# One group of expert tiles, a vector add in the recurrence, and routing one pair later in a two-layer hybrid model

## The chip, the cores and the metric

The kernel runs on one core of a Trainium2 chip. The metric is device time in microseconds (us) of one execution. Three executions took 5005.71, 4992.72 and 5005.48 us, so the median is 5005.48 us. One further execution was profiled; it took 4976.55 us, and its span from the first to the last instruction is 4974.8 us. A profile tells of five engines: PE (TensorE, matrix products), DVE (VectorE), ACT (ScalarE), POOL (GpSimd) and SP (SyncE, which here only issues transfers). PEld is the loading of weights for PE.

## The reference

Sixteen samples go through a tokenizer and two layers; all data are float32, and a row has 256 values. After the tokenizer each sample has 569 tokens (441 from its image, 128 of text).

- Tokenizer: a 2x2 convolution with stride 2, then one attention over 441 image tokens.
- Layer 0: attention in windows of 64 tokens with 8 heads, then a mixture of 8 experts. Each token goes to its two best experts (256 to 512 to 256, with gelu), weighted by the softmax of the router.
- Layer 1: a phasor attention (phases of keys and queries, a running sum over the tokens, a layer norm), then an LSTM of 256 units over the 569 tokens, one after the other, with a gated prefix and suffix sum of its output.

The LSTM is the part that can't be done in parallel over tokens:

```
gates = xp + h @ W_hh.T            # xp = x @ W_ih.T + biases, known for all tokens ahead
i, f, g, o = split(gates, 4)
c = sigmoid(f) * c + sigmoid(i) * tanh(g)
h = sigmoid(o) * tanh(c)
```

## The kernel before, in words

Samples are handled in 8 pairs, `p` = 0 to 7. The 2x569 tokens of a pair fill 9 chunks of 128 rows; chunk `c` and `4 + c` hold the same 128 token times of the two samples, and chunk 8 holds the first 32 and the last 25 tokens of both.

**Tokenizer** (lines 169 to 319), then **windows** (lines 452 to 544). For each pair, rows are normalized and transposed into a tile `xT` (`normed_columns`, line 146), then come Q, K and V (L462 to L488), the attention of each chunk (L495 to L534), and the output row block (L537 to L542). After each pair `send_rows(p)` (line 358) routes its rows: it normalizes again (L141, into `XN` and into `xT`, of which the pool holds one buffer for both uses), forms router scores (L365), ranks them on DVE (L370 to L421), and scatters every row to the two expert regions in HBM by 18 indirect transfers from POOL (L424).

**Experts** (`experts(g)`, line 617). The chunks are dealt into groups: `GROUPS = [[8], [0, 4], [1, 5], [2, 6, 3, 7]]`. In each group every expert's rows are cut into tiles of 256 rows, the number of tiles being a bound that holds for any routing: 15, 23, 23 and 39, so 100 in all. A tile loads its rows and 1154 KB of one expert's weights, transposes (L696, L700), and does two products with gelu between (L707, L713, L717, L722). Its result goes to HBM tensor `YS[g]`.

**Phasors** (`phasors(i)`, line 928) are a generator per pair of chunks: `front` (line 768) gathers the two expert rows of each token (L777, POOL, from `YS` of the group), adds them, normalizes, and forms phases and values; after four pairs a sine on ACT; then `back` (line 839) does the phasor attention, a layer norm, and the LSTM's input part (L916, L920), which goes to the HBM tensor `XPD` of a block. `phasors(8)` does the first 32 tokens and keeps the last 25 for `last_tokens`; `phasors(i)` does the 128 tokens of LSTM block `i + 1`. A `front` or `back` of `phasors(0)` to `phasors(3)` handles two chunks, one of `phasors(8)` and `last_tokens` handles one.

**LSTM** (`lstm(j)`, line 1069). Blocks have 32, 128, 128, 128, 128 and 25 tokens. Eight tokens are a unit: `steps` (line 966) loads `xp` for the unit and runs its 8 steps, and `sums_of` (line 1022) afterwards does the prefix sums and the output of the unit. The four quarters of the units lie in four strips of 32 partitions, so gates are a 128x256 tile. In one step:

1. `begin(t)` (L977): PE multiplies `xp` by the identity into the PSUM tile `g`. It is issued for step `t + 1` right after the recurrent product of step `t`.
2. L989: eight matrix products of `h` with `W_hh` add to it.
3. L996 and L998: ACT reads `g` and makes tanh of the gates.
4. L1000, L1005, L1010, L1012: DVE forms the cell and transposes it and the output gate.
5. L1014: ACT, tanh of the cell. L1015: DVE makes the new `h` (tile `X`). Then step 2 of the next token.

**Order.** A scheduler in the language's library places all instructions ahead of time; each engine then runs its list in order and waits at an instruction until what it needs is there. Steps have high priority, and other work is placed between them. The code says what may lie beside what: `run_all` takes turns between the generators given to it, and what one `run_all` emits may be placed beside the `lstm` emitted next to it.

```
run_all(tiles(0))
run_all((phasors(8), 2 * NP), tiles(1))
lstm(0)
run_all((phasors(0), 2 * NP), tiles(2))
lstm(1)
run_all((phasors(1), 2 * NP), tiles(3))
lstm(2)
```

## Time and profile before

| what | value |
|---|---|
| median of 3 executions | 5005.48 us |
| profiled execution: time, span | 4976.55 us, 4974.8 us |
| PE busy | 3956.3 us, 80% of the span |
| DVE busy | 2287.5 us, 46% |
| ACT, POOL busy | 1173.8 us, 1193.8 us |
| mean granted clock of PE | 0.915 |
| first expert tile done (start of its last add, L722) | 1577.1 us |
| last scatter of rows (L424) begins | 1545.3 us |
| first and last new `h` (L1015) | 2006.0 us, 4876.2 us |

In the page, times are counted from the first instruction. A busy time is the sum over an engine's instructions, and a group's line gives tile names as output, then inputs. The chain of waits is a list of what released what, from the last instruction backwards. PEclk is the share of the full clock that PE was granted. In the list of instructions in order of time, the columns are start, duration, engine, line, operation, output and inputs, and in brackets the idle time before it and what ended it.

### The profile page before, as it was taken

To read this page: it belongs to the slowest core of one execution; us is meant where nothing else is said; L and a number is where in the kernel's file an instruction comes from. 1 tells how busy PE (TensorE), PEld (TensorE's weight loads), DVE (VectorE), ACT (ScalarE), POOL (GpSimd) and SP (SyncE) were. 2 spreads that over 40 slices of the span, in tenths; PEclk is the share of its full clock that TensorE was granted. 3 is DMA by queue.
4 is the path that set the end of the run, shared out by engine and by line. 5 is a ranking of instruction groups with operands and counts; after the bars stand their busy time and mean duration, and the time that the engine had idled before them with its cause. 6 is when DMAs were issued, how large, how long until landed. Compare 5 with 4: busy or idle time off the path is not lost. (4 is left out here: it accounts for less than half of the span.)

```text
span 4974.8 us, 66330 instructions
## 1 busy us (share of the span) xinstructions
PE 3956.3 (80%) x23712; PEld 2468.7 (50%) x23712; DVE 2287.5 (46%) x6971; ACT 1173.8 (24%) x3405; POOL 1193.8 (24%) x1577
## 2 busy tenths in 40 slices
PE   5999877777774898889889999978887888786661
PEld 3555444444444776567555567644444444433330
DVE  3444355555553233533354542355654555444433
ACT  1222233333231221222123222121222122111220
POOL 0000044444443211412141121041413131111212
PEclk8999988888877999999999999989998999999996
DMA  2000000000005664434533344522312222213113
GB/s 73 15 8 8 11 29 29 29 29 29 29 29 187 219 198 143 122 128 154 164 105 99 97 132 168 160 72 56 81 45 72 56 65 53 69 36 82 29 22 75
DMA packets 235928, 399.10 MB, mean 80 GB/s; under 512 B 27744, under 2 KB 204816, under 8 KB 217232
## 3 DMA queue, kind: packets, MB, share of 16 engines
q1 hardware_dynamic: 214592, 348.42, 24.1%
q0 software_dynamic: 13824, 37.77, 2.6%
q10 hardware_dynamic: 7184, 8.67, 0.6%
q8 instruction: 189, 3.10, 0.3%
q14 instruction: 139, 1.14, 0.1%
HBM read 256.51 MB, written 138.25 MB: 79 GB/s over the span
## 5 line engine op out<-in xcount | busy, mean ns | idle before, releaser
L989 PE MATMUL g<-W_hh,X 128*16 128x256 f32 x9088 | 632.5, 398 | 269.5 <-DVE X L1015 267.6
L989 PEld LDWEIGHTS g<-W_hh,X 128*16 128x16 f32 x9088 | 211.9, 98 | 628.9 <-DVE X L1015 465.4
L1000 DVE SCALAR_TENSOR_TENSOR ab<-act 128x128 f32<-128x128 f32 x568 | 188.5, 332 | 673.8 <-ACT act L996 673.2
L707 PE MATMUL hp<-xt,w 128*128 128x256 f32 x1600 | 399.5, 390 | 47.4 <-DVE xt L700 43.3
L977 PE MATMUL g<-xp,ident 128*128 128x256 f32 x1138 | 409.3, 444 | 2.5 <-DMA xp<-XPD 1.6
L996 ACT ACTIVATE act<-g 128x192 f32<-128x192 f32 x568 | 187.5, 330 | 929.2 <-PE g L989 928.6
L717 PE MATMUL y<-w,hT 128*128 128x256 f32 x1600 | 376.9, 380 | 1.3 <-ACT hT L713 1.2
L707 PEld LDWEIGHTS hp<-xt,w 128*128 128x128 f32 x1600 | 296.9, 193 | 103.9 <-DVE xt L700 58.1
L717 PEld LDWEIGHTS y<-w,hT 128*128 128x128 f32 x1600 | 297.4, 190 | 52.8 <-issue 7.9
L977 PEld LDWEIGHTS g<-xp,ident 128*128 128x128 f32 x1138 | 179.8, 195 | 241.7 <-issue 217.3
L916 PE MATMUL xm_False<-W_ih,dxT_False 128*128 128x512 f32 x576 | 276.6, 614 | 8.0 <-ACT dxT_False L908 8.0
L713 ACT ACTIVATE hT<-hp,w 128x256 f32<-128x256 f32 x400 | 168.3, 470 | 475.8 <-PE hp L707 417.4
L1014 ACT ACTIVATE th<-cT 128x32 f32<-128x32 f32 x569 | 130.0, 228 | 613.4 <-DVE cT L1010 601.4
L1049 POOL TENSOR_TENSOR wa<-w,rowA 128x256 f32<-128x256 f32 x72 | 52.6, 731 | 861.5 <-DVE w L1047 861.5
L722 DVE TENSOR_TENSOR ys<-y,w 128x512 f32<-128x512 f32 x100 | 68.8, 688 | 394.4 <-PE y L717 394.2
L777 POOL DMA_INDIRECT yg<-YS,yat x144 | 144.2, 1001 | 352.5 <-DMA YS<-ys 197.3
L524 PE MATMUL ptr<-ident,PB 128*128 128x128 f32 x576 | 105.8, 327 | 119.5 <-POOL PB L517 105.9
L1015 DVE SCALAR_TENSOR_TENSOR X<-toT,th 128x32 f32<-128x32 f32 x569 | 135.7, 238 | 116.0 <-ACT th L1014 114.4
L1005 DVE SCALAR_TENSOR_TENSOR act<-ab 128x64 f32<-128x64 f32 x569 | 172.4, 303 | 14.5
L424 POOL DMA_INDIRECT XS<-XN,at x144 | 139.5, 968 | 114.3 <-DVE ahead L403 70.7
L916 PEld LDWEIGHTS xm_False<-W_ih,dxT_False 128*128 128x128 f32 x576 | 109.2, 195 | 110.5 <-issue 92.3
L524 PEld LDWEIGHTS ptr<-ident,PB 128*128 128x128 f32 x576 | 81.3, 169 | 153.7 <-POOL PB L517 139.7
(304 smaller groups left out, 7099.8 us busy)
## 6 DMA issues: line engine op xcount, KB each, us to landing
w<-in_wpack SPq DMA_DIRECT2D x100, 1154.0 KB
xp<-XPD SPq DMA_DIRECT2D x284, 128.0 KB
XPD<-xps_False SPq DMA_DIRECT2D x64, 512.0 KB
xs<-XS SPq DMA_DIRECT2D x100, 256.0 KB
YS<-ys SPq DMA_DIRECT2D x100, 256.0 KB
XS<-zeros SPq DMA_DIRECT2D x36, 256.0 KB
HD<-h SPq DMA_DIRECT2D x8, 1152.0 KB
fh<-HD SPq DMA_DIRECT2D x72, 128.0 KB
```

Of the source, the lines that this page charges most:

```text
L424: fill(g, nc.gpsimd.indirect_dma_start(out=XS[g], out_offset=bass.IndirectOffsetOnAxis(ap=at[:, i, c : c + 1], axis=0), in_=XN[:, c, :], i ...
L524: nc.tensor.transpose(tr[:, i, :], pb[:, 4 * g + i, :], ident)
L707: nc.tensor.matmul(hp[:, i, :], w1[:, k, hc * 128 : (hc + 1) * 128], xT[:, k, :], start=(k == 0), stop=(k == 1),)
L713: nc.scalar.activation(hT[:, hc, :], hp[:, i, :], AF.Gelu, bias=b1[:, hc : hc + 1])
L717: nc.tensor.matmul(y[:, i, :], hT[:, hc, 128 * i : 128 * i + 128], w2[:, hc, :], start=(hc == 0), stop=(hc == 3),)
L777: nc.gpsimd.indirect_dma_start(out=y, out_offset=None, in_=YS[[g for g in range(NG) if c in GROUPS[g]][0]], in_offset=bass.IndirectOffsetO ...
L916: nc.tensor.matmul(mm, xT[:, k, j * 128 : (j + 1) * 128], Wih[:, k, at_n], start=(k == 0), stop=(k == 1),)
L977: nc.tensor.matmul(gates[t][:, :D], ident, xp[:, t, :], start=True, stop=(j, u, t) == (0, 0, 0))
L989: nc.tensor.matmul(g[32 * q : 32 * q + NB, :D], run["before"][:, k, :], Whh[:, k, q * D : (q + 1) * D], start=False, stop=(k == 1),)
L996: nc.scalar.activation(act[:, :192], g[:, :192], AF.Tanh, scale=0.5)
L1000: nc.vector.scalar_tensor_tensor(ab, act[:, :128].rearrange("p (g x) -> p g x", g=2), 1.0, act[:, 128:].rearrange("p (g x) -> p g x", g=2) ...
L1005: nc.vector.scalar_tensor_tensor(act[:, 192:], ab[:, 1, :], 0.5, ab[:, 0, :], ALU.mult, ALU.add)
```

## The change

Three things are changed.

- `GROUPS` has one group of all 9 chunks. The bound on its tiles is 79. All tiles come first (`finish(experts(0))`), then `phasors(8)`, and the LSTM blocks take turns with `phasors` only.
- The identity product L977 is gone. PE writes only the recurrent product into one of two fixed PSUM tiles `G`; DVE then adds `xp` to it, in two pieces of 192 and 64 columns, into an SBUF tile `gs`, which ACT reads.
- `send_rows` of a pair is emitted after the window attention of the following pair.

```diff
-GROUPS = [[8], [0, 4], [1, 5], [2, 6, 3, 7]]
+GROUPS = [[8, 0, 4, 1, 5, 2, 6, 3, 7]]
...
             nc.sync.dma_start(HD[p], H[p])
-            send_rows(p, wk, ps)
+            if p:
+                send_rows(p - 1, wk, ps)
+        send_rows(NP - 1, wk, ps)
...
+    G = [ps.tile([128, 512], F32, name=f"g{i}") for i in range(2)]
+    for t in G:
+        nc.vector.memset(t, 0.0)
...
-        def begin(t):
-            gates[t] = ps.tile([128, 512], F32, name=f"g{j}_{u}_{t}", tag="g", bufs=2)
-            nc.tensor.matmul(
-                gates[t][:, :D], ident, xp[:, t, :], start=True, stop=(j, u, t) == (0, 0, 0)
-            )
...
-                if run["before"] is not None:
+                step = run["step"]
+                gs = xp[:, t, :]
+                if step:
+                    g = G[step % 2]
                     for k in range(2):
                         for q in range(4):
                             nc.tensor.matmul(
                                 g[32 * q : 32 * q + NB, :D], run["before"][:, k, :],
-                                Whh[:, k, q * D : (q + 1) * D], start=False, stop=(k == 1),
+                                Whh[:, k, q * D : (q + 1) * D], start=(k == 0), stop=(k == 1),
                             )
-                if t + 1 < n:
-                    begin(t + 1)
+                    gs = ls.tile([128, D], F32, name=f"gs{at}", tag="gs", bufs=2)
+                    for lo, hi in ((0, 192), (192, D)):
+                        nc.vector.tensor_tensor(
+                            gs[:, lo:hi], g[:, lo:hi], xp[:, t, lo:hi], ALU.add
+                        )
                 act = run["act"]
-                nc.scalar.activation(act[:, :192], g[:, :192], AF.Tanh, scale=0.5)
+                nc.scalar.activation(act[:, :192], gs[:, :192], AF.Tanh, scale=0.5)
...
-    run_all(tiles(0))
-    run_all((phasors(8), 2 * NP), tiles(1))
+    finish(experts(0))
+    finish(phasors(8))
     lstm(0)
-    run_all((phasors(0), 2 * NP), tiles(2))
-    lstm(1)
-    run_all((phasors(1), 2 * NP), tiles(3))
-    lstm(2)
-    run_all((phasors(2), 2 * NP))
-    lstm(3)
-    run_all((phasors(3), 2 * NP))
-    run_all((last_tokens(), NP))
+    for i in range(4):
+        finish(phasors(i))
+        if i < 3:
+            lstm(i + 1)
+    finish(last_tokens())
```

The last two blocks, `lstm(4)` and `lstm(5)`, stand behind this as before.

## The prediction

> **What bounds the kernel now.** I read the page's shares first, then the starts of L1015 (the new `h`), which cut the span into stages, then the instructions in order of time inside a stage.

> The stages are: windows until 1545 us; expert tiles from 1577; first `h` at 2006, last at 4876; output until 4975. The LSTM's 569 steps take 2870 us, 58% of the span, and the output waits for the last one. A step that has little beside it looks like this:

> ```profile
> 4698.40 1.06 PE L989 MATMUL g<-W_hh,X 128*16 128x256 f32 x16
> ...
> 4699.38 0.70 PE L977 MATMUL g<-xp,ident 128*128 128x256 f32 x2
> ...
> 4699.52 0.33 ACT L996 ACTIVATE act<-g 128x192 f32<-128x192 f32 x1 [1.46 <-PE g L989]
> ...
> 4699.88 0.29 DVE L1000 SCALAR_TENSOR_TENSOR ab<-act 128x128 f32<-128x128 f32 x1 [0.88 <-ACT act L996]
> ...
> 4700.47 0.24 DVE L1010 STREAM_TRANSPOSE cT<-act 128x64 f32<-128x64 f32 x1
> ...
> 4700.81 0.23 ACT L1014 ACTIVATE th<-cT 128x32 f32<-128x32 f32 x1 [0.84 <-DVE cT L1010]
> 4701.07 0.19 DVE L1015 SCALAR_TENSOR_TENSOR X<-toT,th 128x32 f32<-128x32 f32 x1 [0.23 <-ACT th L1014]
> ...
> 4701.32 1.06 PE L989 MATMUL g<-W_hh,X 128*16 128x256 f32 x16 [1.23 <-DVE X L1015]
> ```

> The reader is to see a closed chain of 2.92 us (4698.40 to 4701.32), and that L977 lies in its shadow: ACT starts at 4699.52 while L977 still runs. So L977 costs the chain nothing, although the page gives it much work:

> ```profile
> PEclk8999988888877999999999999989998999999996
> ...
> L989 PE MATMUL g<-W_hh,X 128*16 128x256 f32 x9088 | 632.5, 398 | 269.5 <-DVE X L1015 267.6
> ...
> L977 PE MATMUL g<-xp,ident 128*128 128x256 f32 x1138 | 409.3, 444 | 2.5 <-DMA xp<-XPD 1.6
> ```

> The same step at half clock. First three stretches of the trace (start:end, length, busy time of PE, PEld, DVE, ACT, POOL, then the clock), then the instructions:

> ```profile
> 4680.86:4684.28 3.42, 2.19 (x21) 0.91 (x20) 1.43 (x7) 0.88 (x5) 0.00 (x0) 1.00 0.00 0
> 4684.28:4687.69 3.41, 1.51 (x18) 0.42 (x17) 1.54 (x8) 0.67 (x3) 0.00 (x0) 1.00 0.86 142
> 4687.69:4691.10 3.41, 2.85 (x18) 1.33 (x19) 0.57 (x3) 0.68 (x3) 0.00 (x0) 0.50 0.12 12
> ```

> ```profile
> 4688.25 1.91 PE L989 MATMUL g<-W_hh,X 128*16 128x256 f32 x16 [1.86 <-DVE X L1015]
> ...
> 4690.22 0.33 ACT L996 ACTIVATE act<-g 128x192 f32<-128x192 f32 x1 [2.25 <-PE g L989]
> ```

> The chain to ACT takes 1.97 us instead of 1.12, so a cold step costs 0.85 us more. The clock changes in this trace stand whole multiples of 3.413 us apart. Cut into such stretches, PE busy for 0.25 to 0.40 of a stretch at full clock was followed by half clock 26 times of 26, 0.40 to 0.45 12 of 15, 0.45 to 0.50 9 of 35, over 0.70 never. At half clock it came back only after stretches at least 0.80 busy.

> **The change part by part.**

> *Routing one pair later.* Between a pair's last output row and the next pair's first Q product lie 26.3 us, in which PE waits for the second normalization, then does the router:

> ```profile
> 801.27 0.42 DVE L541 TENSOR_TENSOR o<-ob,rows 128x256 f32<-128x256 f32 x1 [1.13 <-PE ob L537]
> ...
> 806.22 1.94 PE L161 MATMUL b_tr<-ident,XN 128*128 128x128 f32 x8 [4.99 <-DVE XN L141]
> ...
> 827.58 1.65 PE L462 MATMUL q<-a_xT,w_qkv 128*128 128x384 f32 x2 [0.68 <-DVE ahead L405]
> ```

> In the changed kernel's instruction order the previous pair's router products still stand in this place on PE (one `xT` buffer), but their normalization is done; the 10 us of routing on DVE (817 to 828) move into the next window, where a short product waiting for it (L407) holds PE's queue. I take 12 us saved at six boundaries and 20 at the first, 92, less 5 us per pair for about 16 us of DVE work that now stands in the window, 35. At the end two routings and two scatters of 22 us (1523.7 to 1545.3) follow each other on POOL, plus 15. Net -40; bounds -77 (the DVE work costs nothing) and +35 (all 16 us of it show).

> *Tiles.* Alone, a tile takes 8.55 us:

> ```profile
> 1654.07 0.69 DVE L722 TENSOR_TENSOR ys<-y,w 128x512 f32<-128x512 f32 x1 [7.27 <-PE y L717]
> ...
> 1662.62 0.69 DVE L722 TENSOR_TENSOR ys<-y,w 128x512 f32<-128x512 f32 x1 [7.27 <-PE y L717]
> ```

> 15 tiles in a row kept that pace. So the last of 79 comes at 1577 + 78 x 8.55 - 40 = 2204 us. 21 tiles go, which is 180 us less PE work, but 79 now stand ahead of the LSTM instead of 38. On SP, 79 loads instead of 100 and 8 zero fills instead of 32 are hidden by PE at that pace.

> *Ahead of the LSTM.* One tensor `YS` means that the first gather (L777) waits for all tiles; before, `phasors(8)` ran beside 23 tiles. Alone, two-chunk fronts followed each other in 11.7 us (L817 at 3797, 3806, 3820, 3832), and a two-chunk back took 28.5 us (L920 at 3755.7 and 3784.2). One-chunk fronts: 7 us, between half (5.9) and two thirds (7.8) of that. One-chunk backs: between 14 (half) and 21.0 (L896 from 1831 to 1978, tiles between), I take 17.5. With 4 us to the first gather, 12 for the first front, 7 x 7, 4 for the sine and 8 x 17.5, this gives 2413. The order on PE then has four fronts of `phasors(0)` before the first recurrent product: 47. First recurrent product: 2460, where before the first `h` stood at 2006.

> *The step.* The sum leaves PSUM through a DVE add of 192 columns. Nearest rows, both one PSUM and one SBUF operand:

> ```profile
> L488 DVE TENSOR_TENSOR V<-v,rows 128x256 f32<-128x256 f32 x72 | 29.8, 414 | 43.7 <-PE v L484 43.7
> ...
> L849 DVE TENSOR_TENSOR w_False<-sc_False,masks 128x128 f32<-128x128 f32 x72 | 20.2, 281 | 26.0 <-PE sc_False L847 26.0
> ```

> Between 281 and 414 ns, 0.35 us for 192 columns. The hop from DVE to ACT is 0.10 us (L1010 ends 4700.71, L1014 starts 4700.81). So the warm step is 2.92 + 0.45 = 3.37 us, the cold one 4.22. The 64-column add runs while ACT works on the first piece, and the fill of PSUM that goes had no cost.

> *Steps with phasor work beside them.* Before, blocks 1, 2 and 3 took 447.2, 497.4 and 492.5 us for 127 steps, that is 76.4, 126.6 and 121.7 over 127 x 2.92. By the order on PE they contain 4, 8 and 4 fronts, 3, 6 and 8 backs, and 16 `sums_of` each. Three equations give 9.1 us per back, 5.8 per front, 1.6 per `sums_of`; block 4's surplus gives 6 per back of `last_tokens`. Tiles beside the steps cost nothing measurable, so taking them away gains nothing there. In the changed order 319 steps contain 28 backs, 20 fronts, 8 late backs and 40 `sums_of`: 319 x 3.37 + 254 + 115 + 48 + 66 = 1557 us. Phasor work is denser there (8 steps per back instead of 12), so both directions stay open: at the lower end nothing is exposed (-417), at the upper each item costs a third more (+140).

> *A hole.* Ahead of the second step of block 1 the order has four fronts, four backs and four fronts in one piece: 8 x 11.7 + 4 x 28.5 = 208 us.

> *The last 250 steps* have nothing beside them but `sums_of`. PE is busy 1.06 of 3.37 us there, a share of 0.31, where before L977 kept it at 0.6 (first stretch above: 2.19 of 3.42). By the counts above such a stretch always lost the clock, and a cold step (1.91 of 4.22, 0.45) can't win it back. So 250 x 4.22 + 31 x 1.6 = 1106 us.

> [...]

> *Sum.* 2460 + 1557 + 208 + 1106 + 99 (output, 4876 to 4975) = 5430, which is 455 us over the profiled span. That execution lies 29 us under the median, so on the median's scale 5005 + 455 = 5460.

> **The rivals.**

> - *The clock holds in the last 250 steps.* For it: some stretches at 0.45 to 0.50 kept it. Against it: 26 of 26 at 0.25 to 0.40 did not. It takes 212 us off: 5250.
> - *Half of the phasor work hides.* The step now leaves PE 2.3 us instead of 1.2 us beside L977, and the changed order spreads a back evenly over 8 steps. Against it: DVE gets two more instructions per step and its exposed pieces were what made 9.1 us per back. Half of 417 + 208 off: 5150.
> - *It becomes faster.* The same mechanism taken further: phasor work (625 us with the hole) goes under the steps' waits. It decides when more than 455 of the 625, 73%, is hidden. All of it would give 4835. In blocks 2 and 3 before, where tiles were not in the way either, less was hidden.
> - *Denser is worse.* A back of 28.5 us and 8 steps of 27 us wait for each other in order on PE and DVE. At a third more per item, 5600.

> **How the numbers follow.** A change under 0.3% (15 us) can't be told from none. Chances: forecast 0.62 (its own range 5330 to 5590), clock holds 0.13, half hides 0.13, faster 0.05, denser is worse 0.07. The range from 5130 to 5600 takes in the forecast, the first two rivals and part of the last. Only the rival of full hiding is faster: 0.05; 0.01 for the same; 0.94 slower.

> **What would show it.** Right: tiles 8.55 us apart, the last near 2200; first recurrent product near 2460; a hole of some 200 us early in block 1; the last 250 steps 4.2 us apart with clock 0.5 and L988 at 1.9 us (the recurrent product's new line). Wrong: clock 1.0 in those steps; steps under 4 us while backs run beside them; windows that end 100 us earlier.

## The result and the profile after

The changed kernel takes 5520.59 us (median; 5516.41 to 5526.8), the kernel before 4999.1 us in the same comparison (4989.72 to 5005.71). The ratio is 1.1046, with a 95% interval of 1.102 to 1.1071: 521 us slower. The forecast was 5460 in a range of 5130 to 5600. The profiled execution has a span of 5516.2 us.

The page of the changed kernel, with the lines that answer to those shown of before (the recurrent product is now L988, the new add L994):

```profile
PEclk8999998888699999778789888888888555555555
...
L988 PE MATMUL g<-W_hh,X 128*16 128x256 f32 x9088 | 876.6, 522 | 594.9 <-DVE X L1017 593.1
...
L994 DVE TENSOR_TENSOR gs<-g,xp 128x192 f32<-128x192 f32 x1136 | 276.9, 285 | 910.4 <-PE g L988 881.4
L998 ACT ACTIVATE act<-gs 128x192 f32<-128x192 f32 x568 | 206.0, 363 | 1476.4 <-DVE gs L994 1464.2
```

The last nine slices stand at half clock, and the mean recurrent product piece went from 398 to 522 ns. A step of that stretch, in order of time:

```profile
4693.80 0.19 DVE L1017 SCALAR_TENSOR_TENSOR X<-toT,th 128x32 f32<-128x32 f32 x1 [0.23 <-ACT th L1016]
...
4694.05 1.91 PE L988 MATMUL g<-W_hh,X 128*16 128x256 f32 x16 [1.85 <-DVE X L1017]
...
4696.02 0.49 DVE L994 TENSOR_TENSOR gs<-g,xp 128x192 f32<-128x192 f32 x2 [2.03 <-PE g L988]
4696.41 0.36 ACT L998 ACTIVATE act<-gs 128x192 f32<-128x192 f32 x1 [2.65 <-DVE gs L994]
...
4697.99 0.19 DVE L1017 SCALAR_TENSOR_TENSOR X<-toT,th 128x32 f32<-128x32 f32 x1 [0.23 <-ACT th L1016]
```

From one new `h` to the next it is 4.19 us. The add starts 1.97 us after the product (the place where ACT stood in the cold step before), and ACT starts 0.39 us later. The landmarks ahead of that:

```profile
1499.99 0.69 DVE L728 TENSOR_TENSOR ys<-y,w 128x512 f32<-128x512 f32 x1 [12.54 <-PE y L723]
...
2167.22 0.69 DVE L728 TENSOR_TENSOR ys<-y,w 128x512 f32<-128x512 f32 x1 [7.27 <-PE y L723]
...
2432.19 1.06 PE L988 MATMUL g<-W_hh,X 128*16 128x256 f32 x16 [0.40 <-DVE X L1017]
...
2596.32 0.19 DVE L1017 SCALAR_TENSOR_TENSOR X<-toT,th 128x32 f32<-128x32 f32 x1
...
2801.85 0.19 DVE L1017 SCALAR_TENSOR_TENSOR X<-toT,th 128x32 f32<-128x32 f32 x1 [0.17 <-ACT th L1016]
```

They are the first and the last tile, the first recurrent product, and the two ends of the hole in block 1. Block by block (start and end of the stretch, its length, busy time of PE, PEld, DVE, ACT, POOL with counts, then the granted clock):

```profile
2432.00:2597.00 165.00, 122.15 (x732) 55.27 (x732) 92.64 (x347) 32.03 (x110) 35.67 (x59) 0.83 0.18 51
2802.00:3467.00 665.00, 512.62 (x3177) 257.49 (x3178) 389.71 (x1403) 150.99 (x499) 193.49 (x267) 0.85 0.25 66
3467.00:4127.00 660.00, 521.33 (x3215) 260.13 (x3217) 378.91 (x1376) 151.76 (x504) 160.83 (x233) 0.84 0.24 63
4127.00:4284.00 157.00, 114.04 (x728) 48.51 (x720) 84.52 (x330) 24.90 (x101) 33.99 (x76) 0.88 0.16 38
4284.00:5417.00 1133.00, 599.38 (x4381) 209.29 (x4381) 435.22 (x1911) 184.40 (x751) 110.73 (x156) 0.52 0.13 26
```

The first four stretches are the 319 steps with phasor work, the last one the 250 steps without.

### The profile page after: what moved, and what is told of

It is laid out like the page before. It is cut to its first block, busy times and chain, and to the rows that moved or that the text cites. A ratio compares the mean times of both kernels' runs of the same rounds, so it can differ in the third digit from the quotient of the medians.

```text
span 5516.2 us, 62499 instructions
## 1 busy us (share of the span) xinstructions
PE 3943.4 (71%) x21818; PEld 2228.6 (40%) x21818; DVE 2446.7 (44%) x7971; ACT 1174.1 (21%) x3323; POOL 1182.0 (21%) x1577
## 4 chain that ended last, share of the span: by engine, by line
PE 41%; DVE 16%; POOL 7%; issue 6%; ACT 4%; DMA 1%; SPq 0%; POOLq 0%; another core or an unknown queue 0%; DVEq 0%; ACTq 0%
PE g L988 14%; PE hp L713 5%; PE y L723 5%; PE xm_False L922 5%; DVE gs L994 2%; PE po_False L895 2%; DVE ab L1002 2%; ACT act L998 2%; DVE cT L1012 2%; DVE act L1007 1%; ACT th L1016 1%; DVE X L1017 1%; PE fin L1044 1%; POOL XS L424 1%; DVE xt L706 1%
## 5 line engine op out<-in xcount | busy, mean ns | idle before, releaser
L988 PE MATMUL g<-W_hh,X 128*16 128x256 f32 x9088 | 876.6, 522 | 594.9 <-DVE X L1017 593.1
L988 PEld LDWEIGHTS g<-W_hh,X 128*16 128x16 f32 x9088 | 248.1, 115 | 1194.7 <-DVE X L1017 855.7
L994 DVE TENSOR_TENSOR gs<-g,xp 128x192 f32<-128x192 f32 x1136 | 276.9, 285 | 910.4 <-PE g L988 881.4
L998 ACT ACTIVATE act<-gs 128x192 f32<-128x192 f32 x568 | 206.0, 363 | 1476.4 <-DVE gs L994 1464.2
L922 PE MATMUL xm_False<-W_ih,dxT_False 128*128 128x512 f32 x576 | 335.4, 716 | 25.8 <-ACT dxT_False L914 25.8
L713 PE MATMUL hp<-xt,w 128*128 128x256 f32 x1264 | 296.3, 388 | 77.0 <-DVE xt L706 73.6
L713 PEld LDWEIGHTS hp<-xt,w 128*128 128x128 f32 x1264 | 235.4, 191 | 125.2 <-DVE xt L706 92.1
L723 PE MATMUL y<-w,hT 128*128 128x256 f32 x1264 | 285.8, 379 | 0.0
L723 PEld LDWEIGHTS y<-w,hT 128*128 128x128 f32 x1264 | 235.8, 190 | 37.3 <-ACT hT L719 0.4
L1012 DVE STREAM_TRANSPOSE cT<-act 128x64 f32<-128x64 f32 x569 | 137.7, 242 | 14.0
L895 PE MATMUL po_False<-Wo,nT_False 128*128 128x256 f32 x288 | 123.9, 575 | 24.6 <-DVE nT_False L889 24.6
```

Source lines behind the costliest of these rows:

```text
L713: nc.tensor.matmul(hp[:, i, :], w1[:, k, hc * 128 : (hc + 1) * 128], xT[:, k, :], start=(k == 0), stop=(k == 1),)
L723: nc.tensor.matmul(y[:, i, :], hT[:, hc, 128 * i : 128 * i + 128], w2[:, hc, :], start=(hc == 0), stop=(hc == 3),)
L895: nc.tensor.matmul(po[:, j, :], nT[:, k, j * 128 : (j + 1) * 128], l1["Wo"][:, k, :], start=(k == 0), stop=(k == 1),)
L922: nc.tensor.matmul(mm, xT[:, k, j * 128 : (j + 1) * 128], Wih[:, k, at_n], start=(k == 0), stop=(k == 1),)
L988: nc.tensor.matmul(g[32 * q : 32 * q + NB, :D], run["before"][:, k, :], Whh[:, k, q * D : (q + 1) * D], start=(k == 0), stop=(k == 1),)
L994: nc.vector.tensor_tensor(gs[:, lo:hi], g[:, lo:hi], xp[:, t, lo:hi], ALU.add)
```

## The experiments

In all of them the time from the first to the last new `h` is split in two. "Pieces" are waits of over 20 us between two steps; in them the engines do tiles, fronts and backs that stand between LSTM blocks. "Steps" is the rest. The columns are from the profiled executions, the ratio is of medians against the kernel before in the same comparison, where its median lay between 4983 and 4999 us.

| kernel | median us | ratio (95% interval) | first new `h` | pieces | steps |
|---|---|---|---|---|---|
| before | 4999 | 1 | 2006 | 781 | 2089 |
| routing alone | 4896 | 0.9822 (0.9805, 0.984) | 1922 | 777 | 2102 |
| step alone | 5256 | 1.0548 (1.053, 1.0566) | 2006 | 460 | 2684 |
| groups alone | 5125 | 1.0289 (1.0269, 1.0309) | 2520 | 380 | 2112 |
| groups and routing | 5021 | 1.0078 (1.0059, 1.0097) | 2420 | 383 | 2116 |
| changed kernel | 5521 | 1.1046 (1.102, 1.1071) | 2432 | 206 | 2779 |
| changed, 2 products, last 250 steps | 5253 | 1.0537 (1.0516, 1.0558) | 2435 | 206 | 2518 |
| changed, 1 product | 5198 | 1.0423 (1.0399, 1.0446) | 2434 | 231 | 2439 |
| changed, 2 products | 5212 | 1.0451 (1.0427, 1.0475) | 2436 | 309 | 2374 |
| step alone, 2 products, last 193 steps | 5071 | 1.0164 (1.0139, 1.0188) | 2002 | 461 | 2490 |
| step alone, 2 products | 5177 | 1.0367 (1.0345, 1.0389) | 2011 | 723 | 2344 |
| routing, second identity product | 5287 | 1.0609 (1.059, 1.0628) | 1938 | 579 | 2672 |

### The three parts one by one

*Routing alone.*

```diff
-            send_rows(p, wk, ps)
+            if p:
+                send_rows(p - 1, wk, ps)
+        send_rows(NP - 1, wk, ps)
```

> The kernel before with only the routing emitted one pair later. Theory: in the changed kernel the first expert tile is done 77 us earlier (1577.1 to 1499.9 us), and nothing else of the change acts ahead of it. So the routing alone gives these 77 us, all later work keeps its distances, and the time falls from 4999 to some 4920 us (4905 to 4940). Rival: what the windows gain is waited for later (by the first gather or the LSTM's input), and the time stays within 15 us.

It is faster by 1.8%, 91 us by the medians and 76 by the profiled spans. The first tile:

```profile
1492.62 0.69 DVE L724 TENSOR_TENSOR ys<-y,w 128x512 f32<-128x512 f32 x1 [8.64 <-PE y L719]
```

That is 84 us earlier than the 1577.1 of before, and pieces and steps stay within 13 us of before. The gain goes through to the end; the rival falls. The median lies 9 us below the theory's range, while the gain by the spans is the 77 us expected. This version beats both kernels.

*The step alone*: `begin` and its identity product out, the tiles `G` and the DVE add in, as in the diff of the change; groups, order and routing as before.

> The kernel before with only the step changed (identity product gone, DVE adds the input part); groups, order and routing as before. Theory A, chain and clock: 569 steps x 0.45 us = 256 us for the longer chain, and 0.85 us more for each step at half clock. Steps beside tiles keep the clock, those without lose it: at least the 153 of the last two blocks (+130), perhaps most of the block before them as well (+100). So +386 to +490, 5385 to 5490 us. Rival B, chain alone: the clock holds as before, +256, 5255 us. Rival C, the step is harmless and the grouping is what costs: under +100.

270 us, and so below theory A, near B, but not for B's reason. The steps alone grew by 2684 - 2089 = 595 us. Of these, 256 are worked out for the longer chain. The run below that holds the clock in the last 193 steps brings 198 back, so that much is half clock, A's mechanism. The remaining 141 lie in the first 376 steps and are not taken apart: the clock fell there as well (0.87 in block 2), but fronts, backs and tiles that had stood in the pieces also came to lie beside steps. The pieces shrank by 321 us, which neither theory had. Both ends of the wait ahead of block 1's second step, first of before, then of this kernel:

```profile
2133.51 0.19 DVE L1015 SCALAR_TENSOR_TENSOR X<-toT,th 128x32 f32<-128x32 f32 x1 [0.27 <-ACT th L1014]
...
2485.07 0.21 DVE L1015 SCALAR_TENSOR_TENSOR X<-toT,th 128x32 f32<-128x32 f32 x1
```

```profile
2157.56 0.19 DVE L1015 SCALAR_TENSOR_TENSOR X<-toT,th 128x32 f32<-128x32 f32 x1 [0.23 <-ACT th L1014]
...
2454.85 0.19 DVE L1015 SCALAR_TENSOR_TENSOR X<-toT,th 128x32 f32<-128x32 f32 x1 [0.17 <-ACT th L1014]
```

351.6 became 297.3 us. The order tells what moved: the scheduler placed 30 of the 61 later tiles beside steps and 31 between blocks; before it was 16 and 45. With two products more in every step (below) it is 15 and 46 again, so it goes by the PE work in a step.

*Groups alone*: one group of nine chunks, all tiles first; step and routing as before.

> The kernel before with only the groups and the order changed (79 tiles and the first 32 tokens' phasors ahead of the LSTM); step and routing as before. Theory: first recurrent product 77 us later than in the changed kernel, at 2509 us; hole 206; the 319 steps beside phasors take the 1650 us of the changed kernel less 319 x 0.45 = 144 and less some 100 for half clock, so 1405; the last 250 steps 250 x 2.92 + 31 x 1.6 = 780; output 99. Sum 4999, that is +25 on the profiled span of before, 5025 us (4950 to 5100): the late start is paid back by shorter work behind it. Rival: the grouping is the main cost, as its 426 us later start suggests, over 5250 us.

138 us, above the theory's range (25, at most 100) and far below the rival. The first `h` came 514 us later (2006 to 2520; 500 expected), and the pieces shrank by 401. The steps took 2112 us, where the theory's 1405 + 780 makes 2185. What was too small is the sum of the pieces: one hole of 206 was expected from the changed kernel, but with the old step the order has four pieces, 257, 32, 60 and 31 us. That is 174 more, less the 73.

*Groups and routing*, the changed kernel with its step undone.

> The changed kernel with its step undone (identity product again, no DVE add), so groups, order and routing changed. Theory: the sum for groups alone less 77, 4948 us (4870 to 5030), so that the step by itself costs some 570 us of the changed kernel's 5520: 569 x 0.45 = 256 for the chain and 0.85 us for each of nearly 400 steps at half clock. Rival, the step costs only its chain: 5520 - 256 = 5265 us. In both the last 250 steps show a clock near 1.0 and 2.92 us.

34 us slower than before, inside the theory's range but near its upper end, for the same reason. So in the changed arrangement the step costs 497 us (spans of 5516.2 and 5019.1), and its rival of 256 falls. Singly the three parts cost -91 + 270 + 138 = 317 us, together 521. The missing 204 are nearly all in the last two columns: with tiles to place, the step took 321 us out of the pieces; with all tiles ahead of the LSTM it took only 383 - 206 = 177. And its steps grew by 663 instead of 595. That is 144 + 68 = 212.

### The clock

The question is whether the step's price is really PE's clock. The test gives PE work that is read by nobody:

```diff
+                    for _ in range(2 if step >= 319 else 0):
+                        nc.tensor.matmul(
+                            G[(step + 1) % 2][:, D:], ident, xp[:, t, :], start=True, stop=True
+                        )
                     gs = ls.tile([128, D], F32, name=f"gs{at}", tag="gs", bufs=2)
```

> The changed kernel with two identity products per step added behind the recurrent product, in the last 250 steps only; their results are read by nobody, so this is extra work for PE. All engines' order in the first 319 steps is that of the changed kernel. Theory (the clock): PE is then busy 1.06 + 2 x 0.70 = 2.46 of 3.37 us, a share of 0.73, keeps the full clock, and the last 250 steps take 250 x 3.37 + 31 units x 3 = 935 us instead of 1132.6: 5520 - 197 = 5323 us (5300 to 5350). Rival (the slow recurrent product is not a matter of PE's load, or a step of 4.2 us comes from the longer chain): the same 5520 or more, as only work is added.

Adding 500 products made the kernel faster by 258 us (spans of 5516.2 and 5257.7; 268 by the medians). Its stretch of the last 250 steps, and two steps in it:

```profile
4300.00:5160.00 860.00, 575.71 (x5250) 313.04 (x5251) 438.36 (x1867) 180.11 (x733) 108.66 (x152) 1.00 0.16 31
```

```profile
4941.57 1.06 PE L988 MATMUL g<-W_hh,X 128*16 128x256 f32 x16 [1.23 <-DVE X L1021]
4942.56 1.13 PE L993 MATMUL g<-xp,ident 128*128 128x256 f32 x4
4942.69 0.49 DVE L998 TENSOR_TENSOR gs<-g,xp 128x192 f32<-128x192 f32 x2 [1.18 <-PE g L988]
...
4944.91 1.06 PE L988 MATMUL g<-W_hh,X 128*16 128x256 f32 x16 [1.23 <-DVE X L1021]
```

Clock 1.00 instead of 0.52, the product at 1.06 us, and a step of 3.34 us. From step 319 on, the time fell from 1132.6 to 879.5 us, 253 less; the first 319 steps kept theirs (1852.3 and 1844.1). So the missing PE work is shown as the cause there, and the rival falls. The gain is larger than the 197 expected, which puts the run 47 us below its range, because the work of `sums_of` at a unit's end is dearer at half clock too: a unit takes 36 us in the one and 28 in the other, which is more than 8 x 0.85.

*One product in all steps* (`range(1)` without a condition).

> The changed kernel with one identity product per step added in all steps (as much PE work as the kernel before had there, read by nobody). Theory (share of busy time): 1.76 of 3.37 us is 0.52, where the changed kernel's trace lost the clock in 11 of 18 stretches; at half clock 1.91 + 1.22 = 3.13 of 4.2 us is 0.745, below the 0.80 from which it came back. So the clock is still lost in most of the last 250 steps: little gained there (0 to 60 us), some in the 319 steps with phasor work, 5440 us (5350 to 5530). [...]

Here the theory in its narrow form falls: 5198 us, 152 below its range. The last part of the LSTM:

```profile
4440.00:5104.00 664.00, 375.59 (x3477) 167.45 (x3478) 314.70 (x1365) 131.41 (x535) 78.76 (x112) 0.95 0.15 31
```

A steady share of 0.50 kept the clock (1.68 of 3.34 us, as the two products overlap by 0.08): cut into stretches of 3.413 us from 4445 to 5100, those at 0.49 to 0.52 kept it 115 times of 115. It was lost 7 of 13 times at 0.46 to 0.47 and 9 of 29 times at 0.54 to 0.60. All 16 losses lie near the end of a unit, 31 to 55 us apart, and the clock came back after one stretch 14 times of 16 (after four at most), as the products of `sums_of` fill them. So steady steps of this length at this share kept the clock. A statistic over all stretches of a trace, as I had used it, mixes them with uneven ones.

*Two products in all steps.*

> The changed kernel with two identity products per step in all steps (read by nobody). The order on the engines changes with it: before the first step of block 1 stand 7 fronts and 5 backs (4 in the changed kernel), before block 3 three fronts, before block 4 one back, about as in the kernel with groups and routing alone. Theory (clock): outside the pieces between blocks, the steps take the 2116 us of that kernel plus 569 x 0.45 = 256; the pieces about 305; so 2677 us from first to last new h instead of 2985, 5520 - 308 = 5212 us (5150 to 5280). Rival (half clock is not what made the 319 steps with phasor work longer than worked out; the denser work is): only the last 250 steps gain, 197, and the pieces cost 100 more: 5420 us.

The time is the theory's to the microsecond, 5212, and the terms are as well: pieces 309 (305 expected), steps 2374, which is 258 more than with the old step (256 expected). With the clock held (0.93 to 1.00 outside the pieces), the longer chain is all that the steps grew by, 0.45 us x 569. The rival, 5420, falls: half clock cost in the phasor part too (the granted clock there was 0.83 to 0.88 in the changed kernel, and is 0.93 to 0.98 here). Still the version with one product is as fast. It has less warm time but 78 us less in pieces, again by the order.

### What the scheduler places beside a step

Both kernels below have the old groups and routing, the new step, and two products, in the last 193 steps or in all. The first keeps the order of the step alone up to there (30 tiles beside steps), the second has 15 beside steps and 46 between blocks.

> The kernel before with the changed step, and two identity products per step, read by nobody, in the last 193 steps only. All engines' order up to there is that of the kernel with the step alone, which put 30 tiles beside steps and 31 into the pieces between LSTM blocks (before: 16 and 45). Theory: those 193 steps took 879.6 us with the step alone and 3.52 us each where the changed kernel was given the same products, so 193 x 3.52 = 680: 5256 - 200 = 5056 us (5030 to 5085), only 70 over before although every step is 0.42 us longer, because fewer tiles stand between the blocks. Rival: no gain, 5256 us.

> The same with the two products in all 569 steps. By the order on the engines 15 tiles then stand beside steps and 46 between the blocks, as before the change (16 and 45). Theory (the longer step is paid for, or not, by what the scheduler places beside it): the clock holds, steps take 2089 + 569 x 0.45 = 2345 us, the pieces 781 as before, so 4987 + 256 = 5243 us (5190 to 5290), the same time as with the step alone and the clock lost, and 190 more than with the products in the last 193 steps only. Rival (only clock and chain count, the place of the tiles doesn't): 5056 less what half clock still cost in the first 376 steps, under 5056 us.

The first came out as expected, 5071 us (681.5 us for the 193 steps, 680 expected). The second took 5177, 106 more, though it has the full clock in more steps. Its steps took 2344 us (2345 expected), its pieces 723 instead of 781 (341, 307, 75 and none at the four block limits, before 352, 311, 89 and 29), so it came 13 us under the range. Against the first, its pieces are 262 us longer and its steps 146 shorter. The rival falls, as more products made it slower. So the same new step costs 76 or 182 us, according to the place of the tiles.

### A product that was waited for

*Routing, and a second identity product* in the old step, meant to hold the clock there and to move tiles:

```diff
                 if t + 1 < n:
                     begin(t + 1)
+                    nc.tensor.matmul(
+                        g[:, D:], ident, xp[:, t + 1, :], start=True, stop=True
+                    )
```

> The kernel before with routing one pair later and a second identity product per step, read by nobody; step, groups and order as before. Two things should help: by the order on the engines 38 instead of 45 tiles stand in the pieces between LSTM blocks, the others beside steps (7 x 8.55 = 60 us), and the clock of blocks 2 and 3, 0.94, should be full (some 40 steps x 0.85 = 34 us). Theory: 4896 - 94 = 4800 us (4760 to 4870). Rival: 0.70 us of PE work more in each step pushes the phasors' products out of the steps' gaps, and the time rises by up to 569 x 0.1 = 60 us, 4950 us.

5287 us, beyond both theories. The added product (L997) writes the other half of the tile `g` that ACT reads:

```profile
4959.98 1.06 PE L991 MATMUL g<-W_hh,X 128*16 128x256 f32 x16 [1.86 <-DVE X L1020]
...
4960.97 0.70 PE L979 MATMUL g<-xp,ident 128*128 128x256 f32 x2
...
4961.51 0.59 PE L997 MATMUL g<-xp,ident 128*128 128x256 f32 x2
...
4961.94 0.50 PE L1039 MATMUL fin<-W_lin,X 128*128 128x2 f32 x4
4962.14 0.33 ACT L1001 ACTIVATE act<-g 128x192 f32<-128x192 f32 x1 [2.44 <-PE g L997]
```

ACT waits for L997, so both identity products now lie on the chain: at full clock it starts 2.16 us after the recurrent product instead of 1.12, and a step takes 3.95 us instead of 2.92. Nor did the added product hold the clock. Over most of the steps without phasor work PE was granted 0.82 (the number behind the five busy times):

```profile
4500.00:5080.00 580.00, 372.98 (x2635) 183.82 (x2636) 153.15 (x698) 83.14 (x370) 56.45 (x80) 0.82 0.11 19
```

With cold steps among them, the median step of block 5, which has no phasor work, went from 2.92 to 4.64 us. The two pieces fell to 579 us, with 23 tiles beside steps, but that pays for a third of it.

## Why the prediction was right

The sum, term by term, against the changed kernel's trace:

| term | predicted us | measured us |
|---|---|---|
| first recurrent product | 2460 | 2432 |
| 319 steps with phasor work | 1557 | 1647 |
| hole in block 1 | 208 | 206 |
| last 250 steps | 1106 | 1133 |
| output | 99 | 99 |
| sum | 5430 | 5517 |

The forecast of 5460 had 30 us more, for the distance between the profiled execution and the median of before. The changed kernel shows no such distance (5518 and 5521), so the forecast is 61 us short and the sum 87.

*Routing.* The gain was 77 us where -40 was taken, the bound at which "the DVE work costs nothing". The first Q products of the pairs follow each other every 104 us instead of 116, which is the 12 us worked out; the 5 us per pair taken off for DVE did not show. The last window ends 100 us earlier (92 were worked out), and the two routings in a row at the end give back 23 (15 worked out). Windows that end 100 us earlier stood in the prediction as a sign of being wrong, and this part of it was: the 35 us for DVE work are not there. The 37 us are small beside the sum, and the forecast stands by its other terms.

*Tiles and phasors ahead.* The tiles stayed 8.5 to 8.6 us apart to the last, at 2167. Fronts of `phasors(8)` took 6.9 us each (7 taken), backs 18.1 (17.5). The last tile came 37 us earlier than worked out, by the routing, and the phasors behind it took 265 us instead of 256: hence the first product 28 us early.

*The step.* The first piece of the add is done and ACT begins 0.39 us after the add starts, and ACT's instruction is 0.03 us longer from SBUF (0.36 for 0.33): 0.42, where 0.45 was taken. Warm steps took 3.34 us, cold ones 4.19 (3.37 and 4.22 predicted).

*The last 250 steps* lost the clock for good, as forecast (0.52). The rival in which it holds, 5250, is what the run with products in these steps made of it, 5253. Only the price of a unit's end was mis-sized: 31 units at about 2.7 us instead of 1.6.

*The term that was mis-sized* is "319 steps", 90 us too small. Its working gave these steps a warm 3.37 us. By the clock of the four stretches above (0.83 to 0.88), about 505 us of the 1647 ran at half clock; at 5.2 us per step that is 97 steps, and 97 x 0.85 = 82 us. This is an upper estimate, as the blocks from which the prices were worked out had lost some clock themselves (0.94 in blocks 2 and 3 of before). That it was the clock and not denser work is supported by the formula itself (3.34 per step, 9.1 per back, 5.8 per front, 1.6 per unit) for the 127 steps of block 1: with one product it gives 593 us for 10 backs and 9 fronts, measured 589 at clock 0.92; with two products 563 for 8 and 7, measured 554 at clock 0.94; in the changed kernel 623 for 12 backs and 11 fronts, measured 665 at clock 0.85. So the clock is supported as the cause there, not shown apart from the order: no run has the changed kernel's own order with the full clock in this part, as the products put there moved the order.

*The rivals.* "Half of the phasor work hides" and "it becomes faster" fall (steps under 4 us beside backs, their sign, were 29 of the 195 steps of blocks 1 and 2 with a back's products beside them): where the clock was held, a back and a front cost what they had cost before. "Denser is worse" by a third falls for the same reason.

## What to carry to other kernels

Work that lay in the shadow of a chain wasn't free to remove here: in the last steps the granted clock was 0.95 with an identity product of 0.70 us in each step (groups and routing) and 0.52 without it (changed kernel), and there a step at half clock took 4.19 us instead of 3.34. Before taking work off PE, work out which share of the time PE would still be busy. And where a scheduler fills the gaps of a recurrence, look at what a change moves in or out of the gaps: the same step cost 76 or 182 us, according to the place of the tiles, and 497 where there were none to place and the clock was lost.

## What the runs showed of the hardware

Extra matrix products that nobody reads made a kernel 258 us faster: in the last 250 steps of the changed kernel the granted clock was 0.52, with two such products 1.00. In those steps of the changed kernel PE never stood idle for over 2.29 us.

For a steady load of steps of 3.34 us, a PE busy share of 0.50 kept the full clock (1.68 us) and 0.32 lost it (1.06 us). The mean share of a step did not decide alone: in the run with a second identity product in the old step, warm steps of 3.95 us with PE busy for 2.12 (0.54) lost it. A step there is longer than a stretch of 3.413 us, and a stretch that takes in the whole wait of 1.83 us holds only 0.46; from 4450 on, stretches at 0.46 to 0.47 lost the clock 40 times of 50.

From half clock, the full clock came back only after a stretch of at least 0.80 in all four traces that were cut up this way: before (the lowest 0.80), changed (0.84), changed with one product, changed with two in the last 250 steps.

The losses at 0.55 to 0.56 are 9 in the changed kernel with one product (from 4445 on) and 19 in that run (from 4450 on). All 28 stretches hold the four two-column products at the end of a unit (`fin<-W_lin,X`, 0.50 us in the profile). With these left out of PE's busy time, all 75 losses of the two parts lie in stretches under 0.48, and none of the 217 stretches over it lost the clock. No run varied these products, so their part in the losses was not shown.
